# A two-layer graph attention kernel: in layer 1's lightest tiles the norm's mean comes from column sums in the table, the variance from ScalarE, and one row moves from TensorE to VectorE

## The chip, the core and the metric

The program runs on one core of a Trainium2 chip. The metric is the device time of one execution in microseconds (us); lower is better. Several executions are timed and their median is given. The engines are called as the profile calls them: PE (TensorE, matrix products), PEld (its weight loads), DVE (VectorE), ACT (ScalarE), POOL (GpSimd) and SP (SyncE, which only issues DMAs here).

## What is computed

A graph with 10,000 nodes and 170,000 directed edges (80,000 pairs both ways, and one loop per node) goes through two graph attention layers. All numbers are fp32. Layer 1 has four heads of 256 columns, layer 2 one head of 768:

```python
def gat_conv(x, edge_index, W, a_src, a_dst, bias, heads, out_ch, concat):
    xl = (x @ W).reshape(n, heads, out_ch)
    alpha_src = einsum('nhc,hc->nh', xl, a_src)
    alpha_dst = einsum('nhc,hc->nh', xl, a_dst)
    e = leaky_relu(alpha_src[src] + alpha_dst[dst], 0.2)
    e = exp(e - segment_max(e, dst)[dst])
    alpha = e / (segment_sum(e, dst)[dst] + 1e-16)
    return segment_sum(xl[src] * alpha[:, :, None], dst) + bias

h = gat_conv(x, edge_index, W1, a_src1, a_dst1, b1, 4, 256, True)
h = relu(layer_norm(h, g1, be1)) + (x @ Wr1 + br1)
h2 = layer_norm(gat_conv(h, edge_index, W2, a_src2, a_dst2, b2, 1, 768, False), g2, be2)
out = layernorm(x + h2 + (h @ Wr2 + br2))
```

`layer_norm(v, g, b)` is `(v - mean) * rsqrt(var + 1e-5) * g + b` over a node's columns. The change is about the first of the three norms, over 1024 columns.

## The kernel before

**Three stages.** The first stage (lines 590 to 640) makes `table1` in DRAM, one row per node: 1024 columns of `x @ W1` plus `b1`, four destination logits, four source logits, and one number that tells the node's place in the order below. Its loop takes 79 tiles of 128 nodes. For each, PE multiplies (L173), ACT copies the product out of PSUM (L623), DVE multiplies it with the two attention vectors (L626), ACT sums those products by head (L629), POOL adds `b1` (L631) and SP stores the row. A generator, `prepare()`, sorts the nodes by their number of edges in small steps between the tiles. The second stage is layer 1 (`ordered_layer1`), the third layer 2 (`ordered_layer2`).

**Tiles of layer 1.** Nodes are ordered by degree, so each of the 79 tiles of 128 nodes has one number of rows, `SLOTS[t]`: the same number of edges for each of its nodes. Row k of a tile holds, on partition p, the table row of the k-th neighbour of node p. The turns take every second tile from the lightest to the heaviest, then the others back down: 8, 10, 11, 12, 12, 13, 13, 14, 14, 14, 15 (four), 16 (four), 17 (four) and so on up to 26 and 41 rows, then 27 down to 16 (three), 15 (four), 14 (three), 13 (three), 12, 11, 11, 9. In all 1377 rows.

**Gathers.** The rows of a tile are fetched by indirect DMAs that POOL issues (L426), one for each row of 128 nodes, into a ring of 31 rows in SBUF, which is one tile of memory named `ring` in the profile. `ring.fetch` is called as rows are used up, so a row is fetched into the place of the row 31 before it.

**One turn.** The program order is written out by hand (`manual_schedule`), and each engine works through its own part in that order. For tile t:

- Near the end of tile t-1, POOL forms the logits of tile t from the ring (L736) and overwrites the logits in the ring, DVE and ACT turn them into normalised weights `e` (L190, L747, L750, L751, L767, L771 to L773).
- The first `on_pe(t)` rows are PE's: ACT multiplies each by its weights in place (`multiply`, L516, four pieces of 256 columns) and PE adds them up in PSUM with an identity matrix (L728, four records a row). `on_pe` is between 1 and 5: 1 for tiles of up to 13 rows, 2 for 14 and 15, 3 for 16 and 17, 4 for 18 and 19, 5 from 20 on.
- The other rows are DVE's. One in four (the first, the fifth and so on of DVE's rows) DVE weighs itself, with four `scalar_tensor_tensor` of 256 columns (L527). The other three are `shared`: ACT multiplies them (L516, three rows ahead of DVE, `LEAD`), and DVE adds them with one `tensor_tensor` of 1024 columns (L523). Both accumulate in the PSUM tile `acc`; two of these alternate between tiles.
- After the last row comes the norm of tile t, at the head of turn t+1: `deviation` on DVE (two `bn_stats`, L538, one `bn_aggr`, L540) and on ACT (Ln L542, Exp L543, which give 1/sqrt), then on DVE the scaling (L552, L554) and the sum with the residual (L881).
- PE meanwhile transposes x of the tile (L698, copied out by ACT, L699), transposes h of the tile before (L698, L699), multiplies x with `Wr1` (L173) and h with `W2` (L904). ACT copies the last product to `row` (L829) and SP stores it in `table2`.

On PE the order of a turn is therefore L728 (the tile's own rows), L698 (x), L698 (h), L173, L904. On ACT, at the head of a turn, it is Ln, Exp, the two copies L829, the next shared rows, the copies of x, more shared rows, the copies of h.

The function that gives PE its share, and the one that decides which of DVE's rows are shared:

```python
def on_pe(t):
    return min(max(SLOTS[t] // 2 - 5, 1), ON_PE1, SLOTS[t])
...
def shared(t, k):
    return by_vector(t, k) and (k - on_pe(t)) % (SHARE - (len(cuts_of(t)) > 2)) > 0
```

Heavy tiles (22 rows and more) are cut into groups with a running maximum; the change leaves that part as it is.

Of the kernel before, what the change touches and what calls it, by code (L numbers as in the profile page):

```python
# [32 lines left out]
OP = mybir.AluOpType  # L33
# [21 lines left out]
PARTED = 22  # L55

# [25 lines left out]
def gnn_kernel(ctx, tc, x, x_cols, src, dst, src_col, dst_col, W1, a_src1, a_dst1, b1, g1, be1, Wr1, br1,  # L82
# [8 lines left out]
    R1, R2 = C1 + 2 * H1 + 1, C2 + 2 * H2  # L91
# [454 lines left out]
    def scaled(to, parts, mean_and_deviation, g, b):  # L546

        mean, inv = mean_and_deviation
        c = 0
        for a in parts:  # L550
            d = c + a.shape[1]
            nc.vector.scalar_tensor_tensor(to[:, c:d], a, mean, g[:, c:d], op0=OP.subtract, op1=OP.mult)  # L552
            c = d
        nc.vector.scalar_tensor_tensor(to, to, inv, b, op0=OP.mult, op1=OP.add)  # L554
# [13 lines left out]
    with tc.tile_pool(name="w1", bufs=1) as w1p, tc.tile_pool(name="l1", bufs=2) as io, \  # L568
# [22 lines left out]
        nc.scalar.dma_start(b1_b, bass.AP(tensor=b1.tensor, offset=b1.offset, ap=[[0, P], [1, C1]]))  # L591

# [27 lines left out]
        for t in range(NT):  # L620
            p = product(xTs.pop(t), w1, C1)
            row = io.tile([P, R1], F32, name="row")
            nc.scalar.copy(row[:, :C1], p[:, :C1])  # L623
            for i, vec in enumerate((ad_b, as_b)):
                m = io.tile([P, C1], F32, name="scr")
                nc.vector.tensor_mul(m, p[:, :C1], vec)  # L626
                for h in range(H1):
                    s = slice(h * DH1, (h + 1) * DH1)
                    nc.scalar.activation(m[:, s], m[:, s], AF.Copy,  # L629
                                         accum_out=row[:, C1 + i * H1 + h:C1 + i * H1 + h + 1])  # L630
# [45 lines left out]
    def ordered_layer1(mem):  # L676
        nc.scalar.add_instruction(mybir.InstLoadActFuncSet(name=nc.get_next_instruction_name(), act_func_set_id=6, engine=nc.scalar.engine))
        with tc.tile_pool(name="b1", bufs=1) as pool, tc.tile_pool(name="small1", bufs=2) as small, \
# [23 lines left out]
            def from_x(t):  # L702

                xT = pool.tile([P, K0, P], F32, name="xT")
                return xT, halves(xT, xt)

            xt = fetch_x(0)
# [4 lines left out]

            def on_pe(t):


                return min(max(SLOTS[t] // 2 - 5, 1), ON_PE1, SLOTS[t])
# [14 lines left out]
            def summed_logits(lo, hi, ad):  # L731
# [22 lines left out]
            def weights_of(t):  # L754
# [8 lines left out]
                given = summed_logits(at, at + cuts[1], ad)  # L763
# [54 lines left out]

            last = None
# [4 lines left out]
            def store(t):  # L824

                nonlocal full
                row = pool.tile([P, R2], F32, name="row")
# [12 lines left out]
            for t in range(NT + 1):  # L840
# [83 lines left out]
                ahead = iter(())  # L924
                soon = n - LEAD
# [3 lines left out]
                for k in range(n):  # L929
# [20 lines left out]
                    if by_vector(t, k):  # L950
                        weigh(acc, ring.slot(FIRST[t] + k), weights, DH1, shared=shared(t, k))
                    ring.fetch(FIRST[t] + k + 1 + ring.size)
                    due(k)
                due(DEGREES)
                ready += itertools.islice(ahead, max(2 - len(ready), 0))
                last = None
                if live:
                    last = r, acc
# [459 lines left out]
```

## Time and profile before

| | |
|---|---|
| median of three runs | 5525.66 us (5516.87 to 5533.84) |
| the profiled execution | 5484.34 us, span 5482.5 us |
| mean granted TensorE clock in it | 0.944 of full speed |
| instructions | 58273 |
| HBM read, written | 1431.80 MB, 177.29 MB |

The span is the time from the first to the last instruction of the profiled execution. Durations of instructions are read from that execution. The busy digits of the page, in 40 slices of the span (9 is 90% or more), show three stages: the first six slices are the table, the next 18 layer 1, the rest layer 2.

```
DVE  5783343889988888888899995777777777777876
ACT  3434443778889988889888872222222222222322
DMA  4333636899999998999999977988898898888984
```

In a row of the timeline the columns are the start (us), the length, the engine, the line of the kernel, the operation, output and inputs, the shape, and the number of instructions merged; in square brackets stands the time that the engine was idle before, and whom it waited for. A row of groups has the count, then the busy time and the mean length in ns, then the idle time of the engine just before.

### The profile page before, as it was taken

What the parts mean: (1) busy time and instruction counts of PE and PEld (TensorE: products, weight loads), DVE (VectorE), ACT (ScalarE), POOL (GpSimd) and SP (SyncE); (2) the same over time, 40 slices, a digit from 0 to 9 for tenths busy, and PEclk for the clock granted to TensorE, in tenths of its full rate; (3) what the DMA queues carried; (4) which work ended last, traced back from release to release, by engine and by line L of the source; (5) the groups of instructions that cost most, each with busy time, mean ns of one, the idle gap of its engine ahead of it and who ended that gap; (6) DMA issues with size and microseconds to landing.
All of it is one profiled execution on the core that took longest, in us unless ns stands there. A gap on an engine that the chain in (4) does not pass through costs nothing. (4 is left out here: it accounts for less than half of the span.)

```text
span 5482.5 us, 58273 instructions
## 1 busy us (share of the span) xinstructions
PE 4905.3 (89%) x14359; PEld 2707.8 (49%) x14359; DVE 4205.0 (77%) x7341; ACT 2959.9 (54%) x8299; POOL 3341.8 (61%) x3659
## 2 busy tenths in 40 slices
PE   8999995999999987899999997888888888888887
PEld 3444442555544443444445554555555555555554
DVE  5783343889988888888899995777777777777876
ACT  3434443778889988889888872222222222222322
POOL 2446455566667766677676644666666666666663
PEclk9999997999999998999999999989999998988898
DMA  4333636899999998999999977988898898888984
GB/s 156 121 101 90 92 94 216 312 340 363 366 369 377 379 351 291 348 360 384 372 370 363 351 268 261 327 315 309 311 323 313 305 318 304 300 300 301 315 307 168
DMA packets 474303, 1591.30 MB, mean 290 GB/s; under 512 B 118327, under 2 KB 122487, under 8 KB 473958
## 3 DMA queue, kind: packets, MB, share of 16 engines
q0 software_dynamic: 322384, 1286.62, 65.0%
q1 hardware_dynamic: 149520, 297.43, 16.2%
q10 hardware_dynamic: 2054, 3.42, 0.2%
q8 instruction: 122, 2.00, 0.1%
q14 instruction: 223, 1.83, 0.1%
HBM read 1431.80 MB, written 177.29 MB: 293 GB/s over the span
## 5 line engine op out<-in xcount | busy, mean ns | idle before, releaser
L426 POOL DMA_INDIRECT ring<-table,slots x2675 | 2661.1, 995 | 1515.9 <-issue 641.3
L516 ACT ACTIVATE ring<-ring,e 128x256 f32<-128x256 f32 x4232 | 1740.4, 507 | 87.3 <-DVE e L773 49.3
L527 DVE SCALAR_TENSOR_TENSOR acc<-ring,e,acc 128x256 f32<-128x256 f32 (+1 forms) x2574 | 1600.5, 622 | 161.4 <-PE acc L728 72.5
L523 DVE TENSOR_TENSOR acc<-acc,ring 128x1024 f32<-128x1024 f32 x781 | 961.7, 1231 | 66.9 <-ACT ring L516 12.0
L1064 PE MATMUL big<-wr,w 128*128 128x512 f32 (+1 forms) x2464 | 874.6, 499 | 129.8 <-issue 128.0
L1019 PE MATMUL big<-ring,diagonals 128*128 128x256 f32 x2754 | 743.7, 427 | 184.1 <-issue 151.2
L173 PE MATMUL big<-w,xT 128*128 128x512 f32 x1896 | 824.0, 596 | 23.0 <-DMA w<-in_W_dram 10.1
L904 PE MATMUL half<-w,hT 128*128 128x512 f32 (+1 forms) x2528 | 830.4, 486 | 0.0
L173 PE MATMUL big<-wr,xT 128*128 128x512 f32 x1896 | 830.0, 594 | 0.2 <-ACT xT L699 0.2
L1018 ACT ACTIVATE diagonals<-ident,e 128x128 f32<-128x128 f32 x1377 | 422.9, 390 | 641.9 <-PE big L1019 176.2
L1019 PEld LDWEIGHTS big<-ring,diagonals 128*128 128x128 f32 x2754 | 585.6, 216 | 343.2 <-issue 230.4
L1064 PEld LDWEIGHTS big<-wr,w 128*128 128x128 f32 x2464 | 479.9, 196 | 495.6 <-issue 465.8
L904 PEld LDWEIGHTS half<-w,hT 128*128 128x128 f32 x2528 | 477.7, 189 | 372.8 <-issue 331.7
L728 PE MATMUL acc<-ring,ident 128*128 128x512 f32 x1108 | 522.2, 618 | 107.9 <-ACT ring L516 59.8
L173 PEld LDWEIGHTS big<-w,xT 128*128 128x128 f32 x1896 | 361.4, 191 | 481.1 <-issue 463.0
L173 PEld LDWEIGHTS big<-wr,xT 128*128 128x128 f32 x1896 | 355.4, 191 | 418.2 <-issue 417.6
L542 ACT ACTIVATE sd<-mv,eps 128x1 f32<-128x1 f32 x237 | 70.0, 296 | 748.6 <-DVE mv L540 314.6
L728 PEld LDWEIGHTS acc<-ring,ident 128*128 128x128 f32 x1108 | 212.9, 196 | 372.0 <-issue 208.4
L626 DVE TENSOR_TENSOR scr<-big,ad_b 128x1024 f32<-128x1024 f32 x79 | 96.7, 1225 | 374.7 <-ACT row L623 350.9
L631 POOL TENSOR_TENSOR row<-row,none 128x1024 f32<-128x1024 f32 x79 | 187.2, 2370 | 261.4 <-ACT row L623 259.5
L629 ACT ACTIVATE scr<-scr 128x256 f32<-128x256 f32 x632 | 254.5, 404 | 120.3 <-DVE scr L626 120.3
L623 ACT COPY row<-big 128x1024 f32<-128x1024 f32 x79 | 79.7, 1009 | 312.8 <-issue 283.6
(193 smaller groups left out, 3392.8 us busy)
## 6 DMA issues: line engine op xcount, KB each, us to landing
ring<-table,slots POOLq DMA_INDIRECT x2675
table<-row SPq DMA_DIRECT2D x79, 516.0 KB
h_d<-hT SPq DMA_DIRECT2D x79, 512.0 KB
w<-h_d SPq DMA_DIRECT2D x77, 512.0 KB
table<-row SPq DMA_DIRECT2D x79, 385.0 KB
ring<-table SPq DMA_DIRECT2D x79, 385.0 KB
xT<-in_x_cols_dram SPq DMA_DIRECT2D x79, 384.0 KB
x_d<-xt SPq DMA_DIRECT2D x79, 384.0 KB
```

The costliest lines, as they stand in the source:

```text
L173: nc.tensor.matmul(p[:, c:e], aT[:, j, :], w[:, j, c:e], start=(j == 0), stop=(j == k - 1))
L426: nc.gpsimd.indirect_dma_start(out=to, out_offset=None, in_=table, in_offset=bass.IndirectOffsetOnAxis(ap=index, axis=0), **more)
L516: nc.scalar.activation(row[:, s], row[:, s], AF.Copy, scale=e[:, h:h + 1])
L523: nc.vector.tensor_add(acc[:, :c], acc[:, :c], row[:, :c])
L527: nc.vector.scalar_tensor_tensor(acc[:, s], row[:, s], e[:, h:h + 1], (acc if first is None else first)[:, s], op0=OP.mult, op1=OP.add)
L629: nc.scalar.activation(m[:, s], m[:, s], AF.Copy, accum_out=row[:, C1 + i * H1 + h:C1 + i * H1 + h + 1])
L631: nc.gpsimd.tensor_add(row[:, :C1], row[:, :C1], b1_b)
L728: nc.tensor.matmul(acc[:, c:c + BANK], ident, ring.slot(q + k)[:, c:c + BANK], start=(k == 0), stop=(k == m - 1))
L904: nc.tensor.matmul(q, hT[:, j, :], w2[:, j, c:c + q.shape[1]], start=(j == 0), stop=(j == K1 - 1))
L1018: nc.scalar.activation(diagonals[:, (k - lo) % G, :], ident, AF.Copy, scale=e[:, k - lo, :])
L1019: nc.tensor.matmul(to, diagonals[:, (k - lo) % G, :], ring.slot(at + k)[:, ON_PE2:C2], start=False, stop=(k == n - 1), skip_group_check=True)
L1064: nc.tensor.matmul(r[:, c:d], hT[:, j, :], wr2[:, j, c:d], start=False, stop=(j == K1 - 1 and d < C2), skip_group_check=True)
```

## The change

It sets `LIGHTER = 18` and calls a tile *lighter* when it has fewer than 12 rows, or 12, 14 or 16. There are 22 of them: seven of 16 rows, six of 14, three of 12, three of 11, and one each of 10, 9 and 8. Three things change.

1. **The table's rows carry four more columns**, the sums of the row's 256 columns for each head. In the first stage ACT's one copy out of PSUM becomes four, each with an accumulator output, and POOL adds the sums of `b1` to them. A row grows from 1033 to 1037 numbers (4132 to 4148 bytes).
2. **In lighter tiles the norm changes.** POOL copies the sums of a tile's rows out of the ring before they are overwritten, multiplies them by the weights (`mean_begun`), and half way through the tile ACT sums them up to minus the mean (`minus_mean`). After the last row ACT squares `acc` with this mean as bias and sums that up (`deviation_from`), then takes Ln and Exp as before. `bn_stats` and `bn_aggr` fall away. The squares themselves are not needed; they are written over the space of xT and row, which now share one tile of memory, `both`.
3. **In lighter tiles PE gets one row less**, which may leave none. Where none is left, DVE's first row starts the sum with `tensor_scalar` (which does not read `acc`).

```diff
-    R1, R2 = C1 + 2 * H1 + 1, C2 + 2 * H2
+    R1, R2 = C1 + 3 * H1 + 1, C2 + 2 * H2
...
-            nc.scalar.copy(row[:, :C1], p[:, :C1])
+            for h in range(H1):
+                s = slice(h * DH1, (h + 1) * DH1)
+                nc.scalar.activation(row[:, s], p[:, s], AF.Copy,
+                                     accum_out=row[:, C1 + 2 * H1 + h:C1 + 2 * H1 + h + 1])
...
             nc.gpsimd.tensor_add(row[:, :C1], row[:, :C1], b1_b)
+            nc.gpsimd.tensor_add(row[:, C1 + 2 * H1:R1 - 1], row[:, C1 + 2 * H1:R1 - 1], b1_sums)
...
-                xT = pool.tile([P, K0, P], F32, name="xT")
...
+            both = pool.tile([P, D0 + R2], F32, name="both")
+            xT, row, squares = both[:, :D0].rearrange("p (k n) -> p k n", n=P), both[:, D0:], both[:, :C1]
...
+            def lighter(t):
+
+                return SLOTS[t] < LIGHTER and (SLOTS[t] < 12 or SLOTS[t] % 2 == 0)
...
-                return min(max(SLOTS[t] // 2 - 5, 1), ON_PE1, SLOTS[t])
+                return min(max(SLOTS[t] // 2 - 5 - lighter(t), 0), ON_PE1)
...
+                    if sums is not None:
+                        nc.gpsimd.tensor_copy(sums[:, a - lo:b - lo], rows[:, :, C1 + 2 * H1:C1 + 3 * H1])
                     nc.gpsimd.tensor_scalar(slots[:, a:b], rows[:, :, R1 - 1], -1.0, float(NP), op0=OP.mult, op1=OP.min)
                     nc.gpsimd.memset(rows[:, :, C1 + H1:], -BIG)
...
+            def mean_begun(t, e):
+
+                nc.gpsimd.tensor_tensor(sums_of_rows[t], sums_of_rows[t], e, op=OP.mult)
+
+            def minus_mean(t):
+
+                sums = sums_of_rows.pop(t).rearrange("p k h -> p (k h)")
+                mean = small.tile([P, 1], F32, name="mean")
+                nc.scalar.activation(sums, sums, AF.Copy, scale=-1.0 / C1, accum_out=mean)
+                return mean
+
+            def deviation_from(mean, a):
+
+                sd = small.tile([P, 1], F32, name="sd")
+                nc.scalar.activation(squares, a, AF.Square, bias=mean, accum_out=sd)
+                nc.scalar.activation(sd, sd, AF.Ln, scale=1.0 / C1, bias=eps)
+                nc.scalar.activation(sd, sd, AF.Exp, scale=-0.5)
+                return sd
...
-                    r_before, means = last
-                    stats = deviation(small, pieces(means[:, :C1], BANK))
+                    r_before, means, minus = last
+                    if minus is None:
+                        stats = deviation(small, pieces(means[:, :C1], BANK))
+                    else:
+                        stats = minus, deviation_from(minus, means[:, :C1])
...
-                    scaled(h, [means[:, :C1]], stats, g1_b, be1_b)
+                    scaled(h, [means[:, :C1]], stats, g1_b, be1_b, OP.subtract if minus is None else OP.add)
...
+                minus = None
+                if t in sums_of_rows:
+                    mean_begun(t, es[0][0])
...
-                    if by_vector(t, k):
+                    if not k and by_vector(t, k):
+                        for h in range(H1):
+                            s = slice(h * DH1, (h + 1) * DH1)
+                            nc.vector.tensor_scalar(acc[:, s], ring.slot(FIRST[t])[:, s], weights[:, h:h + 1], None,
+                                                    op0=OP.mult)
+                    elif by_vector(t, k):
                         weigh(acc, ring.slot(FIRST[t] + k), weights, DH1, shared=shared(t, k))
                     ring.fetch(FIRST[t] + k + 1 + ring.size)
                     due(k)
+                    if k == n // 2 and t in sums_of_rows:
+                        minus = minus_mean(t)
```

More of the change, by code (lines that the diff above doesn't have):

```diff
@@ L55 @@
 PARTED = 22
+LIGHTER = 18
 def chunk_counts(n_edges):
@@ L551, in scaled @@
             d = c + a.shape[1]
-            nc.vector.scalar_tensor_tensor(to[:, c:d], a, mean, g[:, c:d], op0=OP.subtract, op1=OP.mult)
+            nc.vector.scalar_tensor_tensor(to[:, c:d], a, mean, g[:, c:d], op0=centre, op1=OP.mult)
             c = d
@@ L591, in gnn_kernel @@
         nc.scalar.dma_start(b1_b, bass.AP(tensor=b1.tensor, offset=b1.offset, ap=[[0, P], [1, C1]]))
+        b1_sums = w1p.tile([P, H1], F32, name="b1_sums")
+        nc.vector.reduce_sum(b1_sums, b1_b.rearrange("p (h d) -> p h d", d=DH1), axis=AX.X)
         def weight_steps():
@@ L762, in weights_of @@
                     nc.gpsimd.tensor_copy(ad, own)
-                given = summed_logits(at, at + cuts[1], ad)
+                if lighter(t):
+                    sums_of_rows[t] = small.tile([P, LIGHTER, H1], F32, name="sums", bufs=1)[:, :n]
+                given = summed_logits(at, at + cuts[1], ad, sums_of_rows.get(t))
                 yield
@@ L826, in store @@
                 nonlocal full
-                row = pool.tile([P, R2], F32, name="row")
                 for c, q in full:
@@ L957, in ordered_layer1 @@
                 if live:
-                    last = r, acc
+                    last = r, acc, minus
             store(NT - 1)
```

6 lines of the change are left out of this document (4 added, 2 removed).

## The prediction

> **What bounds the kernel now.** I read the three stages first (the windows view, one row per stage), then single turns of layer 1 in the same view, then the waits, then the timeline of two turns.
>
> ```profile
> PE 4905.3 (89%) x14359; PEld 2707.8 (49%) x14359; DVE 4205.0 (77%) x7341; ACT 2959.9 (54%) x8299; POOL 3341.8 (61%) x3659
> ```
> ```profile
> 0.00:877.00 877.00, 841.59 (x1961) 371.33 (x1961) 482.08 (x979) 355.43 (x1370) 422.00 (x326) 0.99 0.38 107
> 877.00:3320.00 2443.00, 2269.77 (x6582) 1159.29 (x6583) 2126.80 (x3174) 2002.55 (x5064) 1588.32 (x1956) 0.98 0.94 347
> 3320.00:5482.00 2162.00, 1793.93 (x5817) 1177.21 (x5815) 1596.14 (x3188) 601.95 (x1866) 1331.43 (x1377) 0.89 0.86 301
> ```
>
> Columns: stretch, its length, then busy time of PE, PEld, DVE, ACT, POOL, the granted clock, DMA share, GB/s. The first stage (the table) is PE alone: 842 of 877 us. Layer 1, 2443 us, is where the change works; there PE, DVE and the DMA engines are all over 85%, so the averages decide nothing. Layer 2 is untouched. Single turns of layer 1, of 13, 14, 15, 16 and (near the end) 12 rows, cut where L881 ends:
>
> ```profile
> 1074.80:1099.50 24.70, 24.24 (x74) 12.78 (x73) 23.17 (x34) 21.48 (x55) 14.83 (x18) 1.00 0.92 338
> 1099.50:1125.70 26.20, 25.74 (x79) 13.59 (x78) 23.20 (x33) 21.26 (x55) 15.86 (x19) 1.00 0.93 344
> 1206.80:1233.60 26.80, 25.83 (x78) 13.59 (x78) 25.11 (x38) 21.86 (x56) 17.64 (x24) 1.00 0.94 347
> 1314.40:1342.50 28.10, 27.64 (x84) 14.39 (x83) 25.32 (x38) 22.99 (x60) 19.04 (x25) 1.00 0.97 364
> 3227.90:3251.20 23.30, 22.84 (x68) 12.11 (x68) 21.83 (x33) 17.03 (x44) 13.80 (x17) 1.00 0.87 307
> ```
>
> From 13 to 14 rows the turn grows by 1.5 us while DVE's work does not grow (23.17, 23.20); from 14 to 15 DVE grows by 1.9 and the turn by 0.6. So two clocks run side by side and the later one sets each turn. The waits of DVE in two 14-row turns, then in three 16-row turns (total, times, longest):
>
> ```profile
> DVE acc L527 <- PE acc L728: 3.1, 2, 1.6
> ```
> ```profile
> DVE acc L527 <- PE acc L728: 3.2, 3, 1.1
> ```
>
> Even sizes wait for TensorE's sum of its own rows (L728): 1.57 us a turn at 14 rows, 1.07 at 16. The 15-row turns have no such wait. Without the wait DVE alone would need 26.3 - 1.57 = 24.75 us (14 rows), 28.0 - 1.07 = 26.93 (16), 24.65 (13), 26.8 (15), 23.3 (12): I call this DVE's clock. PE's clock follows from its timeline in a 14-row turn:
>
> ```profile
> 1123.66 3.60 PE L728 MATMUL acc<-ring,ident 128*128 128x512 f32 x8
> 1127.10 0.82 PE L698 MATMUL half<-ident,xt 128*128 128x128 f32 x6
> 1128.37 1.09 PE L698 MATMUL half<-ident,h 128*128 128x128 f32 x8 [0.46 <-ACT xT L699]
> ```
>
> Two rows take 1127.10 - 1123.66 = 3.44 us, so one row 1.72. PE's clock is 26.3 us with two rows; hence 24.6 with one, 28.0 with three, and 22.9 with none if only PE's own work counted.
>
> **The change part by part.** 22 turns are "lighter": 7 of 16 rows, 6 of 14, 3 of 12, 3 of 11, one each of 10, 9 and 8. Each loses one PE row: -1.72 us of PE.
>
> *The row goes to DVE.* By the sharing rule (every fourth DVE row is weighed by DVE itself, the others are weighed by ScalarE and only added), the extra row is an added one for 16, 12, 11, 10 and 8 rows, and a weighed one for 14 and 9. Their prices stand in the 13-row turn:
>
> ```profile
> 1074.75 2.06 DVE L527 SCALAR_TENSOR_TENSOR acc<-ring,e,acc 128x256 f32<-128x256 f32 x4
> 1076.90 3.88 DVE L523 TENSOR_TENSOR acc<-acc,ring 128x1024 f32<-128x1024 f32 x3
> ```
>
> Weighed: 2.06 us. Added: 3.88 / 3 = 1.29.
>
> *The norm leaves DVE, partly.* The end of a 14-row turn on DVE, and ACT beside it:
>
> ```profile
> 1117.55 2.49 DVE L523 TENSOR_TENSOR acc<-acc,ring 128x1024 f32<-128x1024 f32 x2
> 1120.07 1.30 DVE L538 BATCH_NORM_STATS2 st<-acc 128x6 f32<-128x512 f32 x2
> 1121.72 1.28 DVE L552 SCALAR_TENSOR_TENSOR h<-acc,mv,g 128x1024 f32<-128x1024 f32 x1
> 1123.11 1.28 DVE L554 SCALAR_TENSOR_TENSOR h<-h,sd,be 128x1024 f32<-128x1024 f32 x1
> 1124.50 1.22 DVE L881 SCALAR_TENSOR_TENSOR h<-h,big 128x1024 f32<-128x1024 f32 x1
> 1127.30 1.01 DVE L527 SCALAR_TENSOR_TENSOR acc<-ring,e,acc 128x256 f32<-128x256 f32 x2 [1.57 <-PE acc L728]
> ```
> ```profile
> 1117.71 3.31 ACT L516 ACTIVATE ring<-ring,e 128x256 f32<-128x256 f32 x8 [1.16 <-DVE total L772]
> 1121.65 0.30 ACT L542 ACTIVATE sd<-mv,eps 128x1 f32<-128x1 f32 x1 [0.62 <-DVE mv L540]
> 1121.98 0.20 ACT L543 ACTIVATE sd<-sd 128x1 f32<-128x1 f32 x1
> ```
>
> From the last add (1120.04) to L552 are 1.68 us of statistics. They go. In their place ScalarE squares acc, and the question is whether L552, which reads the same acc, may run beside it. The first stage answers by analogy: DVE's L626 and ACT's L623 both only read the product, and L626 needs nothing that L623 writes.
>
> ```profile
> 604.74 0.40 ACT L629 ACTIVATE scr<-scr 128x256 f32<-128x256 f32 x1
> 605.05 0.19 ACT L629 ACTIVATION_READ_ACCUMULATOR scr<-scr 128x1 f32 x1
> 609.92 1.01 ACT L623 COPY row<-big 128x1024 f32<-128x1024 f32 x1 [4.68 <-issue]
> ```
> ```profile
> 610.97 1.22 DVE L626 TENSOR_TENSOR scr<-big,ad_b 128x1024 f32<-128x1024 f32 x1 [7.94 <-ACT row L623]
> ```
> ```profile
> L802 ACT COPY ring<-acc 128x1024 f32<-128x1024 f32 x13 | 13.1, 1006 | 14.5 <-remote 8.4 <-PE half L904 4.3 <-PE acc L728 1.2
> ```
>
> L626 starts 0.04 after L623 ends: two engines' reads of one PSUM tile are put one after the other. So L552 will wait for the square. Its length is not in the trace; bounds are 1.01 (the copy of acc, L802) and 1.3 (that plus a separate accumulator read of 0.19 and 0.1 more for a bias held per partition, the difference of L542 and L543). I take 1.11 + 0.09 for the end of the read + 0.07 for two handovers: L552 starts 1.27 after the last add instead of 1.68. **DVE gains 0.41 us, not 1.68.** The deviation (0.30 + 0.20) is ready before L552 ends. If L552 need not wait, L554 would wait for it instead, at about 1.85 + 0.1: a gain of 1.1. The other end, a square that starts late because ACT is still weighing rows, is a rival below.
>
> The Trainium skill, "PSUM — Partial Sum Buffer", section "PSUM bank collisions raise a hardware error", says that accesses by two engines to one bank collide, reads against reads included, so software has to keep them apart. By it L552 waits, as in the L626 row; it speaks against the reading that the whole of the statistics comes off DVE. By it layer 1 comes out at +1.6 (below), without it at -8.0.
>
> *Tiles of 12 rows and under: no PE row is left.* What then follows the big product L904 on PE is the transposition of x, whose copies ACT makes. From the 13-row turn, where one row is left (L904 ends as L728 starts):
>
> ```profile
> 1072.79 1.88 PE L728 MATMUL acc<-ring,ident 128*128 128x512 f32 x4
> 1075.79 1.09 PE L698 MATMUL half<-ident,h 128*128 128x128 f32 x8 [0.46 <-ACT xT L699]
> ```
> ```profile
> 1072.99 0.38 ACT L829 COPY row<-half 128x258 f32<-128x258 f32 x1 [1.23 <-PE half L904]
> 1073.26 1.71 ACT L516 ACTIVATE ring<-ring,e 128x256 f32<-128x256 f32 x4
> 1075.15 0.86 ACT L699 COPY xT<-half 128x512 f32<-128x512 f32 x2 [0.17 <-PE half L698]
> ```
>
> ACT stands idle only 0.17 us before the xT copies: copy, four multiplications (row 1 now, row 2 before) and xT copies stay in this order. So without L728 the copies come only 0.17 earlier, and PE's clock goes from 24.6 to 24.4, not to 22.9.
>
> *The sum for layer 1*, later clock of the two, in us:
> 16 rows: PE 28.0 to 26.3, DVE 26.93 + 1.29 - 0.41 = 27.81; 28.02 to 27.81 = -0.2, x7 = -1.5.
> 14 rows: PE 26.3 to 24.6, DVE 24.75 + 2.06 - 0.41 = 26.4; +0.1, x6 = +0.6.
> 12 and under: DVE at most 23.5 + 0.9 = 24.4, PE 24.6 to 24.4; -0.17, x9 = -1.5.
> That is -2.4. But several light turns run on DVE's clock already, because PE had a lead when they came (the 12-row turn of 23.30 above); there the dearer DVE turn counts in full. Carrying both clocks through the 78 turns in order (rows start when L881 and L728 are done; the transposition of h starts when L881 and PE's own work are done) gives **+1.6**; with no gain on DVE at all it gives +7.9, with 1.1 of gain -8.0, and without the ACT chain at 1.1 -16.6.
>
> *The table.* Four pieces with accumulator (4 x 0.40 + 0.09) replace one copy of 1.01: 0.7 us later for L626, hidden behind DVE's 7.94 us of idle time, except for the last tile, whose row layer 1 awaits: **+0.7**. The sum of b1 lies in DVE's idle time before its first product. *Rows of 4148 bytes instead of 4132*, 0.39%, count where the DMA engines are full, in the two stretches of 17 to 21 rows:
>
> ```profile
> 1399.00:1891.60 492.60, 475.38 (x1389) 242.56 (x1388) 438.82 (x617) 437.08 (x1107) 346.01 (x410) 1.00 0.99 374
> 2401.20:2887.30 486.10, 470.59 (x1381) 240.65 (x1379) 437.81 (x619) 432.16 (x1098) 343.94 (x406) 1.00 1.00 377
> ```
>
> PE is 97% busy in both, so 0 if PE sets them and 0.39% of 979 = 3.8 if the DMA engines do; I take **+1**. The outer bound is 0.39% of 2443 = 9.5. *POOL*: a copy and a product a light turn, some 0.3 us each, inside this gap at the turn's head or beside the gathers:
>
> ```profile
> 1126.29 1.00 POOL L426 DMA_INDIRECT ring<-table,slots  x1 [4.46 <-issue]
> ```
>
> Nothing; without that cover 22 x 0.6 = 13. The mean on ACT (some 0.4 us) lies in its idle time. **Sum: +1.6 + 0.7 + 1 = +3 us** on the profiled 5484.3, 5488. That execution is 41 us under the median of the runs, 5525.7; for the median I forecast 5529.
>
> **The rivals.**
> *DVE has room and the whole PE row comes off.* 22 turns at up to 1.72, carried through: -35 us, 5491. For it: PE is the later clock in the even sizes. Against it: 15-row turns, with two PE rows and 25.11 us of DVE, take 26.8, so the 16-row turn with two PE rows cannot take 26.3. Chance 0.14.
> *The square comes late (slower).* ACT is in order, and at the end of a turn it weighs the next turn's PE rows: in the 14-row turn those eight end at 1121.02, 0.98 after the last add. Beyond 1.68 - 1.27 = 0.41 of lateness the new norm costs DVE more than the old. At 1.4 of lateness each light turn loses 1.0 against before plus its row: carried through, +26, with the rest 5554. Against it: one PE row less is four weighings (1.65 us) less in just that place. Chance 0.13.
> *xT, row and squares share one tile.* If the xT copies had to wait for the store of row that was issued just before them, every turn of the 78 would be late by at least that store:
>
> ```profile
> table<-row SPq DMA_DIRECT2D x79, 385.0 KB
> ```
>
> At 344 GB/s 1.1 us, so +87 or more, 5613. Against it: the gathers wait for single slots of the ring, which is one tile too. Chance 0.03.
>
> **How the numbers follow.** Forecast 5529, chance 0.70; its own range, from the bounds of -8 and +8 and 9 us of scatter between runs, is 5515 to 5545. The range that should hold 8 in 10 also takes in half of each near rival: 5508 to 5552. Less than 0.3% (16.6 us) is about what a measurement of this kernel can tell from no change; so faster 0.14, same 0.70, slower 0.16.
>
> **What would show it.** In the profile after: L527's wait for L728 gone or under 0.4 us in 14- and 16-row turns; 14-row turns still near 26.3, 16-row turns near 27.8; L552 preceded by a wait for the square of about 1.2 us; in turns of 11 and 12 rows ACT without a gap before the xT copies; layer 2 unchanged. I am wrong if L552 starts right behind the last add, if a light turn falls below 25.5 (14) or 27 (16), or if heavy turns, which the change does not touch, get longer by more than 0.1 us.

## The result and the profile after

| | before | after |
|---|---|---|
| median of 22 runs each | 5525.74 us | 5535.95 us |
| lowest and highest | 5512.24, 5540.83 | 5528.04, 5550.54 |
| the profiled execution | 5484.34 us | 5532.32 us |

The ratio is 1.0020, 95% interval 1.0013 to 1.0027: the change costs about 10 us (7 to 15). The two profiled executions lie 48 us apart, but that is no measure of the change: that of before lies 41 us under its median, that of after 4 us. Layer 2, whose code is unchanged, is some 20 us longer in the second (2163.7 us before, 2183.7 after, from the last L881 or L920 on; the profiles of the eight runs on one chip below lie between 2157.7 and 2175.5). So sizes of whole stages are taken from medians, and the traces are used for what is the same in every turn.

The windows view of the three stages after (stretch, length, busy time of PE, PEld, DVE, ACT, POOL, granted clock, DMA share, GB/s):

```profile
0.00:890.00 890.00, 843.35 (x1958) 371.68 (x1961) 482.86 (x977) 396.73 (x1914) 436.21 (x403) 0.99 0.38 105
890.00:3345.50 2455.50, 2237.80 (x6492) 1144.73 (x6493) 2125.70 (x3153) 2016.24 (x5132) 1608.69 (x2009) 0.97 0.94 346
3345.50:5530.40 2184.90, 1818.08 (x5819) 1192.24 (x5817) 1598.08 (x3190) 597.88 (x1866) 1332.67 (x1377) 0.88 0.85 298
```

In layer 1 PE has lost 32 us of work (2269.77 to 2237.80: 22 rows of 1.72 would be 38) and DVE has gained none on balance (2126.80 to 2125.70), yet the stage is not shorter: in this profile it is 12 us longer, chiefly in turns that the change does not touch (see the bytes and POOL, below). In the first stage ACT has grown by 41 us (355.43 to 396.73), and the first turn of layer 1 ends 13 us later (L920 at 964.4; L881 at 951.1 before). That end alone is no measure: among the runs below it comes between 955.7 and 961.2 in the five whose first stage has the tile period of before, and at 973.3 in the run of the table alone. PE's waits in the middle of that stage (40 to 270 us; waiting line, what it waited for, total, times, longest), before and then after:

```profile
PE big L173 <- PE big L173: 6.6, 8, 0.9
...
PE big L173 <- DVE scr L626: 1.0, 1, 1.0
```
```profile
PE big L174 <- DVE scr L632: 16.1, 11, 1.5
```

After, PE waits there for DVE to finish with a product (L632), 1.5 us a tile. Before it waited 0.9 a tile; the profile puts one of those nine waits down to DVE (L626) and eight to PE's own product before. The prediction put no cost on that stage but the last tile.

Single turns of layer 1 after: 13, 14, 15 and 16 rows.

```profile
1088.40:1113.00 24.60, 24.14 (x77) 12.85 (x76) 23.11 (x35) 19.72 (x51) 15.36 (x20) 1.00 0.92 339
1139.80:1166.20 26.40, 24.21 (x74) 12.75 (x74) 23.56 (x35) 21.00 (x56) 17.02 (x21) 1.00 0.93 325
1219.90:1246.70 26.80, 25.81 (x78) 13.59 (x78) 25.11 (x38) 21.02 (x54) 16.98 (x23) 1.00 0.95 337
1328.20:1356.00 27.80, 27.49 (x78) 14.43 (x78) 24.87 (x36) 23.38 (x60) 19.15 (x27) 0.94 0.98 360
```

The 14-row turn takes 26.4 and the 16-row turn 27.8. The turns of 13 and 15 rows, which the change leaves alone, stand where they were (24.6, 26.8). The end of a 14-row turn on DVE, and ACT beside it:

```profile
1132.39 2.06 DVE L528 SCALAR_TENSOR_TENSOR acc<-ring,e,acc 128x256 f32<-128x256 f32 x4
1135.77 1.28 DVE L553 SCALAR_TENSOR_TENSOR h<-acc,mean,g 128x1024 f32<-128x1024 f32 x1 [1.32 <-ACT both L851]
...
1138.56 1.22 DVE L920 SCALAR_TENSOR_TENSOR h<-h,big 128x1024 f32<-128x1024 f32 x1
1139.70 0.48 DVE L528 SCALAR_TENSOR_TENSOR acc<-ring,e,acc 128x256 f32<-128x256 f32 x1
```
```profile
1134.54 1.11 ACT L851 ACTIVATE both<-acc,mean 128x1024 f32<-128x1024 f32 x1 [1.53 <-PE half L943]
1135.55 0.19 ACT L851 ACTIVATION_READ_ACCUMULATOR both<-acc,mean 128x1 f32 x1
```

The square (L851) takes 1.11 us and starts 0.09 after DVE's last row (1134.45); ACT had been idle for 1.53, so it is not late (the bracket names PE's L943, but the start fits the end of DVE's row). L553 (L552 before) waits for it: 1.32 us instead of 1.68 of statistics. Right behind L920 the next tile's rows start without a gap: the wait for PE's sum is gone.

### The profile page after: what moved, and what is told of

The parts are those of the page before. It is cut to its first block, busy times and chain, and to the rows that moved or that the text cites. A ratio compares the mean times of both kernels' runs of the same rounds, so it can differ in the third digit from the quotient of the medians.

```text
span 5530.4 us, 58913 instructions
## 1 busy us (share of the span) xinstructions
PE 4899.2 (89%) x14268; PEld 2708.6 (49%) x14271; DVE 4206.6 (76%) x7319; ACT 3010.9 (54%) x8912; POOL 3377.6 (61%) x3789
## 5 line engine op out<-in xcount | busy, mean ns | idle before, releaser
L528 DVE SCALAR_TENSOR_TENSOR acc<-ring,e,acc 128x512 f32<-128x512 f32 (+1 forms) x2566 | 1596.4, 622 | 124.7 <-PE acc L740 31.5
L524 DVE TENSOR_TENSOR acc<-acc,ring 128x1024 f32<-128x1024 f32 x796 | 980.2, 1231 | 89.9 <-ACT ring L517 27.3
L1068 PE MATMUL big<-ring,diagonals 128*128 128x256 f32 x2754 | 759.6, 433 | 198.3 <-issue 173.6
L174 PE MATMUL big<-wr,both 128*128 128x512 f32 x1896 | 838.6, 599 | 0.2 <-ACT both L706 0.2
L943 PE MATMUL half<-w,hT 128*128 128x512 f32 (+1 forms) x2528 | 830.5, 486 | 0.0
L943 PEld LDWEIGHTS half<-w,hT 128*128 128x128 f32 x2528 | 477.5, 189 | 373.1 <-issue 334.8
L174 PEld LDWEIGHTS big<-wr,both 128*128 128x128 f32 x1896 | 359.0, 193 | 423.8 <-issue 423.1
L740 PE MATMUL acc<-ring,ident 128*128 128x512 f32 x1020 | 474.9, 612 | 69.0 <-ACT ring L517 48.6
L632 DVE TENSOR_TENSOR scr<-big,ad_b 128x1024 f32<-128x1024 f32 x79 | 96.7, 1224 | 371.6 <-ACT row L628 264.3
L740 PEld LDWEIGHTS acc<-ring,ident 128*128 128x128 f32 x1020 | 193.2, 194 | 310.6 <-issue 171.3
L628 ACT ACTIVATE row<-big 128x256 f32<-128x256 f32 x316 | 116.5, 382 | 286.6 <-issue 245.8
```

Source lines behind the costliest of these rows:

```text
L174: nc.tensor.matmul(p[:, c:e], aT[:, j, :], w[:, j, c:e], start=(j == 0), stop=(j == k - 1))
L524: nc.vector.tensor_add(acc[:, :c], acc[:, :c], row[:, :c])
L528: nc.vector.scalar_tensor_tensor(acc[:, s], row[:, s], e[:, h:h + 1], (acc if first is None else first)[:, s], op0=OP.mult, op1=OP.add)
L740: nc.tensor.matmul(acc[:, c:c + BANK], ident, ring.slot(q + k)[:, c:c + BANK], start=(k == 0), stop=(k == m - 1))
L943: nc.tensor.matmul(q, hT[:, j, :], w2[:, j, c:c + q.shape[1]], start=(j == 0), stop=(j == K1 - 1))
L1068: nc.tensor.matmul(to, diagonals[:, (k - lo) % G, :], ring.slot(at + k)[:, ON_PE2:C2], start=False, stop=(k == n - 1), skip_group_check=True)
```

## The experiments

Two theories stood against each other. **First stage:** the cost comes from the four copies with accumulator, which stand in a ring of waits between DVE and ACT. **Light turns:** it comes from the turns of layer 1, where the row costs DVE more than the norm gives back. A third one, the longer rows of the table, was tried by itself. Ratios are to the kernel before on the same chip; 0.0010 is 5.5 us.

**The table alone: no tile is lighter.** The sums are made and stored, and nobody uses them; the shared tile `both` stays.

```diff
-LIGHTER = 18
+LIGHTER = 0
...
-                return min(max(SLOTS[t] // 2 - 5 - lighter(t), 0), ON_PE1)
+                return min(max(SLOTS[t] // 2 - 5, 1), ON_PE1, SLOTS[t])
```

> The changed kernel with no lighter tile: the table keeps its four sum columns, ACT keeps the four pieces with accumulator, xT and row keep their shared tile, and layer 1's turns are those of before. Theory (the first stage pays): in the profile of the changed kernel the end of the first L881 (there L920) came 13 us later than before, because in the stretch where DVE also searches the sorted list, the tile's period grew from 11.45 to 12.01 us: ACT's copy out of PSUM lies on the chain there. Then this run should be 8 to 13 us over before, with the first turn's end at 964, and light turns as before (14 rows at 26.3, 16 at 28.0). Rival (the lighter turns pay, the first stage is scatter): within 3 us of before, and the period in that stretch back at 11.45.

Measured: 5507.94 against 5490.89, 1.0026 (1.0014 to 1.0039): +14 us (8 to 21). PE's waits in its first stage are those of after:

```profile
PE big L174 <- DVE scr L632: 16.1, 11, 1.5
```

That is about the whole of the change's cost, and a little over the range expected. The first turn ends at 973.3, later than the 964 expected.

**The longer rows alone.** The kernel before with rows of 4148 bytes, the four new columns filled with zeros by POOL.

```diff
-    R1, R2 = C1 + 2 * H1 + 1, C2 + 2 * H2
+    R1, R2 = C1 + 3 * H1 + 1, C2 + 2 * H2
...
+            nc.gpsimd.memset(row[:, C1 + 2 * H1:R1 - 1], 0.0)
```

> Before with rows of 4148 bytes, the four new columns set to zero and not used. Theory (the gathers' bytes cost next to nothing): first stage as before, layer 1 longer by 0 to 4 us, in all 0 to +4. Rival (the longer rows are what made turns 38 to 50 some 10 us longer in the changed kernel's profile): +8 to +12, in the turns of 20 rows and more.

Measured: 5494.74 against 5490.89, 1.0009 (0.9998 to 1.0020). The bytes cannot be told from nothing; up to 11 us are not excluded by this ratio alone. But the two stretches of 17 to 21 rows, where the DMA engines are full and longer rows would show first, hold still:

```profile
1407.30:1899.50 492.20, 475.87 (x1390) 242.76 (x1389) 438.69 (x617) 435.81 (x1109) 347.76 (x410) 1.00 0.99 376
2409.80:2897.10 487.30, 470.72 (x1381) 240.52 (x1379) 437.83 (x619) 430.97 (x1098) 345.25 (x407) 1.00 0.99 377
```

492.2 and 487.3 us, against 492.6 and 486.1 before.

**The sums off the chain.** After, but the copy is one again, and ACT forms the sums from the finished row, behind POOL's addition of `b1`; so POOL's addition of the sums of `b1` falls away.

```diff
-            for h in range(H1):
-                s = slice(h * DH1, (h + 1) * DH1)
-                nc.scalar.activation(row[:, s], p[:, s], AF.Copy,
-                                     accum_out=row[:, C1 + 2 * H1 + h:C1 + 2 * H1 + h + 1])
+            nc.scalar.copy(row[:, :C1], p[:, :C1])
...
+            for h in range(H1):
+                s = slice(h * DH1, (h + 1) * DH1)
+                nc.scalar.activation(m[:, s], row[:, s], AF.Copy,
+                                     accum_out=row[:, C1 + 2 * H1 + h:C1 + 2 * H1 + h + 1])
```

> The changed kernel, but the first stage has its one copy out of PSUM back; the sums are formed by ACT afterwards, from the row with b1 already added, in four passes with accumulator behind the sums of the logits. ACT has 0.65 us more to do in each of the 79 tiles than in the changed kernel. Theory (only the place on the chain mattered): the period in the search stretch is 11.45 again, the first turn ends at 951 to 953, and the time is 8 to 12 us under the changed kernel: -2 to +4 against before. Rival (ACT's load or POOL's extra work mattered, not the chain): no better than the changed kernel, +10.

Measured: 5496.08 against 5490.89, 1.0016 (1.0002 to 1.0029). PE's waits are back to the pattern of before, although ACT does more work here than in after:

```profile
PE big L174 <- PE big L174: 6.5, 8, 0.9
...
PE big L174 <- DVE scr L627: 1.0, 1, 1.0
```

So it was the place of the pieces that cost, not their amount. What is left, 9 us by the ratio (1 to 16) and 5 by the medians, is the light turns' share and the bytes. Both lie over the -2 to +4 expected, which the interval does not rule out.

**The row alone.** The kernel before with `lighter` and the row moved, and the norm as before.

```diff
-                return min(max(SLOTS[t] // 2 - 5, 1), ON_PE1, SLOTS[t])
+                return min(max(SLOTS[t] // 2 - 5 - lighter(t), 0), ON_PE1)
...
-                    if by_vector(t, k):
+                    if not k and by_vector(t, k):
+                        for h in range(H1):
+                            s = slice(h * DH1, (h + 1) * DH1)
+                            nc.vector.tensor_scalar(acc[:, s], ring.slot(FIRST[t])[:, s], weights[:, h:h + 1], None,
+                                                    op0=OP.mult)
+                    elif by_vector(t, k):
```

> Before with one row moved from PE to DVE in the 22 lighter tiles, and the norm and table as before. Theory (two clocks, DVE's is the later once the row is moved): 16-row turns at 26.93 + 1.29 = 28.2 us, 14-row turns at 24.75 + 2.06 = 26.8, 12-row turns at 24.6; carried through all turns +8 us. Rival (PE is the bound and DVE has room): 16 rows at 26.8, 14 rows at 25, in all -15 to -35.

Measured: 5495.70 against 5490.89, 1.0011 (0.9999 to 1.0022), +6 us (-1 to 12). The turns are the better witness, a 14-row and a 16-row one:

```profile
1130.00:1156.80 26.80, 24.30 (x74) 12.75 (x74) 25.11 (x39) 19.56 (x51) 16.84 (x19) 1.00 0.93 324
1319.40:1347.60 28.20, 25.89 (x78) 13.50 (x78) 26.42 (x40) 22.78 (x60) 19.14 (x24) 1.00 0.99 359
```

DVE is 1.6 us busier in the first than in after (25.11 against 23.56), and the turn is 0.4 longer: that is what the new norm is worth, because 1.32 of the 1.68 us remain as a wait.

**The norm alone**, on the kernel with the sums off the chain: `on_pe` as before, the norm as after.

```diff
-                return min(max(SLOTS[t] // 2 - 5 - lighter(t), 0), ON_PE1)
+                return min(max(SLOTS[t] // 2 - 5, 1), ON_PE1, SLOTS[t])
```

> As e3 (sums off the chain), but with PE's rows as before: only the norm of the lighter tiles is changed. Theory (two clocks; in even sizes PE is the later one): 14-row turns stay at 26.3 and 16-row turns at 28.0, because the 0.4 us off DVE is spent waiting for L728; carried through all turns -1 us in layer 1, so 0 to +4 against before with the first stage of e3. Rival (the statistics are worth their 1.5 us wherever they go): 22 x 1.5 = -33.

Measured: 5496.52 against 5490.93, 1.0006 (0.9995 to 1.0018). DVE's waits in turns 1 to 17, before and then here:

```profile
DVE acc L527 <- PE acc L728: 18.3, 11, 4.7
```
```profile
DVE acc L528 <- PE acc L738: 18.2, 12, 4.8
DVE h L553 <- issue: 8.9, 5, 2.1
```

With PE's row in its place PE still sets these turns, so nothing that the norm does on DVE can count. And L553 waits 2.1 us in a 14-row turn. The profile names no releaser for that wait ("issue"), but L553 starts at 1132.08, 0.03 after the end of the accumulator read behind the square. The square is late there, on ACT:

```profile
1127.65 3.31 ACT L517 ACTIVATE ring<-ring,e 128x256 f32<-128x256 f32 x8 [0.99 <-DVE e L787]
1130.86 1.10 ACT L849 ACTIVATE both<-acc,mean 128x1024 f32<-128x1024 f32 x1
```

Eight weighings for PE's two rows hold it up by 0.8 us. This is the second rival's late square, hidden here behind PE; in after the row's move takes four of the eight away.

**Two halves, swapped between the engines.** On the kernel with the sums off the chain: ACT squares the first 512 columns while DVE scales the last 512, then they change places.

```diff
-                nc.scalar.activation(squares, a, AF.Square, bias=mean, accum_out=sd)
...
+                nc.scalar.activation(squares[:, lo], a[:, lo], AF.Square, bias=mean, accum_out=first)
+                nc.vector.scalar_tensor_tensor(to[:, hi], a[:, hi], mean, g1_b[:, hi], op0=OP.add, op1=OP.mult)
+                nc.scalar.activation(first, first, AF.Identity, scale=1.0 / C1, bias=eps)
+                nc.scalar.activation(squares[:, hi], a[:, hi], AF.Square, bias=mean, accum_out=sd)
+                nc.vector.scalar_tensor_tensor(to[:, lo], a[:, lo], mean, g1_b[:, lo], op0=OP.add, op1=OP.mult)
+                nc.scalar.activation(sd, sd, AF.Ln, scale=1.0 / C1, bias=first)
...
-                    scaled(h, [means[:, :C1]], stats, g1_b, be1_b, OP.subtract if minus is None else OP.add)
...
+                        nc.vector.scalar_tensor_tensor(h, h, inv, be1_b, op0=OP.mult, op1=OP.add)
```

> As e3, but ACT squares the first half of acc (one PSUM bank) while DVE scales the second half, and then the other way round; the two sums are put together with one more ACT instruction of one column. Theory (L552 waits because both engines would read one bank): DVE's wait of 1.32 us before L552 falls under 0.2, a shorter wait of about 0.7 appears before L554, a 14-row turn falls from 26.43 to 26.1 and a 16-row turn from 27.80 to 27.5; 6 us under e3. Rival (the tile as a whole is what is guarded, or the wait is for the deviation): the wait stays at 1.3 or moves to L554 in full, time as e3.

Measured: 5505.39 against 5490.93, 1.0032 (1.0022 to 1.0043), and a miss: slower than with whole squares, by 9 us. DVE and ACT at the end of a 16-row turn:

```profile
1317.17 0.75 DVE L852 SCALAR_TENSOR_TENSOR h<-acc,mean,g 128x512 f32<-128x512 f32 x1 [0.91 <-ACT both L851]
```
```profile
1316.36 0.69 ACT L851 ACTIVATE both<-acc,mean 128x512 f32<-128x512 f32 x1
1316.95 0.19 ACT L851 ACTIVATION_READ_ACCUMULATOR both<-acc,mean 128x1 f32 x1
...
1318.01 0.69 ACT L854 ACTIVATE both<-acc,mean 128x512 f32<-128x512 f32 x1 [0.54 <-DVE h L852]
```

DVE's L852 reads columns 512 to 1023, ACT's L851 the others, and L852 still starts 0.02 us after the accumulator read behind L851 (1316.95 + 0.19 = 1317.14, and 1317.17). The two reads of one tile are put one after the other whether they touch the same columns or not, and now there are two such handovers a turn. The 14-row turn goes from 26.4 to 27.1, the 16-row turn from 27.8 to 28.5. The Trainium skill, "PSUM — Partial Sum Buffer", section "PSUM bank collisions raise a hardware error", says that engines on different banks do not collide; the halves of `acc` are 2048 bytes each, one bank by that page. By it the halves could run side by side; here the program waited for the tile as a whole, 0.91 us, and no run shows whether the chip needed it.

**The step moved.** The kernel before, with the generator's step of a tile put behind the copy instead of at the end of the tile. So ACT's sum of a weight product (L609) comes behind the copy (L623) in ACT's order.

```diff
             nc.scalar.copy(row[:, :C1], p[:, :C1])
+            if t:
+                next(steps, None)
...
-            next(steps, None)
```

> Before, with one change of order in the first stage: the sorting and weight steps are issued after the next tile's copy out of PSUM instead of ahead of it. ACT's copy then no longer queues behind the weight step's sum (0.86 us), which waits for DVE. Theory (DVE's step, ACT's sum, ACT's copy and DVE's product are one ring, and its length sets the stretch): the period of 14 tiles falls from 11.45 to 10.3 to 10.6, 12 to 16 us under before. Rival (DVE's own work sets the stretch, 11.45 is its busy time): no change, within 3 us of before.

Measured: 5470.63 against 5490.93, 0.9957 (0.9941 to 0.9973): 20 us faster than before (15 to 32), by the line order alone, and more than the 12 to 16 expected. ACT and PE in that stretch:

```profile
160.71 1.01 ACT L623 COPY row<-big 128x1024 f32<-128x1024 f32 x1 [4.69 <-issue]
161.62 0.85 ACT L609 ACTIVATE scr<-scr 128x768 f32<-128x768 f32 x1
```
```profile
149.74 24.62 PE L173 MATMUL big<-w,xT 128*128 128x512 f32 x57
```

57 matrix products without a gap, 24 a tile: 10.3 us a tile instead of 11.45.

**Everything together:** sums off the chain, the step moved, the halves, and in tiles without a PE row ACT's shared rows behind the copies of x.

```diff
-                multiplied(first + 2)
+                if not live or first:
+                    multiplied(first + 2)
```

> The changed kernel with the sums off the chain (e3), the halves swapped (e6), the steps moved (e7), and in tiles without a PE row the copies of x ahead of the weighing of row 1 on ACT. Expected by the chain theory: e3's first stage less 12 to 16, layer 1 less 6 for the halves and less 3 for the order (PE's wait of 1.6 us for the copies of x gone in the tiles of 12 rows and under, whose turns come to 23 to 24): 12 to 20 us under before. By the rivals above: as e3.

Measured: 5490.35 against 5490.93, 0.9998 (0.9986 to 1.0010). A miss (12 to 20 us under before were expected), and most of it follows from the two runs before it: the kernel with the halves lay 14 us over before, and the step gains 20. The new order on ACT did little: PE's wait for the copies of x in the last turns falls from 7.4 us to 0.5, but turns 62 to 78 take 442.0 us against 443.2 with the halves alone.

**The norm on the odd sizes.** The norm alone and the step moved, with the tiles of 13, 15 and 17 rows as the lighter ones; PE keeps its rows.

```diff
-                return SLOTS[t] < LIGHTER and (SLOTS[t] < 12 or SLOTS[t] % 2 == 0)
+                return SLOTS[t] in (13, 15, 17)
```

> The norm change where DVE's clock is the later one: tiles of 13, 15 and 17 rows get the mean from the sums and the squares on ACT, all tiles keep PE's rows of before; sums off the chain and steps moved as in e3 and e7. Theory (each DVE-bound turn gets the 0.36 us that the norm really saves, until PE's clock holds it): 15-row turns from 26.81 to 26.45, 17-row turns from 28.19 to about 28.0, 13-row turns stay at 24.6; layer 1 -4 us, with e7's first stage 20 to 26 us under before. Rival (the norm is worth the whole of its statistics): 15-row turns at 26.3 and 17-row turns at 28.0 as well, since PE holds both, so the two differ only in the 15-row turn by 0.15 us.

Measured, on another chip, where before takes 5162.02: 5142.58, 0.9963 (0.9949 to 0.9976). A turn of 15 rows, which runs on DVE's clock:

```profile
2938.50:2964.90 26.40, 25.84 (x78) 13.59 (x78) 23.56 (x35) 22.77 (x59) 18.73 (x27) 1.00 0.98 358
```

26.4 where the run below, on the same chip with these turns unchanged, takes 26.8: DVE has 1.6 us less work (25.11 there) and the turn gets 0.4 of it. The 17-row turns come to 27.95, about the 28.0 expected. The time is 19 us under before where 20 to 26 were expected. The step alone gave the same ratio within its interval, so nothing is measurable beyond that.

**After with the step moved**, behind its four pieces.

```diff
                                      accum_out=row[:, C1 + 2 * H1 + h:C1 + 2 * H1 + h + 1])
+            if t:
+                next(steps, None)
...
-            next(steps, None)
```

> The changed kernel with one change of order in the first stage, the steps issued after the next tile's pieces (as e7). The four pieces with accumulator stay. Theory (the pieces cost only because they stand in the ring of step, sum, copy and product): the stretch runs at 10.3 us a tile, the first turn ends at 938 to 942 instead of 964, and what is left against before is e7's gain plus the lighter turns' +6: 8 to 16 us under before. Rival (four pieces and POOL's additions load the stage in any order): a period over 10.6 and a time at or over before.

Measured, on the same chip as the run before: 5142.03 against 5162.02, 0.9962 (0.9949 to 0.9976). That is 20 us under before (12 to 26), more than the 8 to 16 expected. The change itself, with one call moved, beats the kernel before by as much as that call alone does without the change. Its 15-row turn, and PE's waits between 40 and 270 us, which have no line of DVE's products left; the line shown is the only wait of a table product:

```profile
2941.30:2968.10 26.80, 25.80 (x78) 13.59 (x78) 25.11 (x39) 21.08 (x55) 17.22 (x23) 1.00 0.99 370
```
```profile
PE big L174 <- ACT row L617: 1.0, 1, 1.0
```

So the four pieces are free once nothing waits behind them in a ring, as the first theory says. What the light turns cost (below) is smaller than the width of the two intervals and cannot be read from these two ratios.

## Why the prediction was right in its range and wrong in its reason

The time forecast, 5529, lies 7 us under the 5536 measured; the change costs 10 us where +3 was said. The turns of 14 and 16 rows came out as worked out; the larger part of the cost came from a place that the prediction called hidden. So the time fell into the range of 5515 to 5545 partly by luck: that range was made for doubts about layer 1 and for scatter between runs, and had nothing in it for this place.

**The two clocks: right.** Forecast 26.4 us for 14 rows and 27.81 for 16; measured 26.4 and 27.8 in the rows above. The row's prices on DVE (2.06 weighed, 1.29 added) hold: with the row alone the turns are 26.8 and 28.2, and 24.75 + 2.06 = 26.81, 26.93 + 1.29 = 28.22. The rival in which the whole PE row comes off is dead.

**L552 waits for the square: right.** 1.27 was said, 1.32 measured. So DVE gains 0.36 us, not 0.41, and the 15-row turn of the odd-size run shows just that. The late square did not come: ACT was idle before it in the 14-row turn above, since the row's move had taken its four weighings away from there, as the prediction argued; without the move it was late. The shared tile held nothing up either: the 13- and 15-row turns are unchanged.

**Twelve rows and under: the mechanism right, the sum too small.** ACT goes through copy, shared rows and copies of x without a gap, and PE waits for it, as said. In a turn of 11 rows on ACT, then PE:

```profile
1013.44 0.38 ACT L865 COPY both<-half 128x258 f32<-128x258 f32 x1 [2.89 <-PE half L943]
1013.71 1.71 ACT L517 ACTIVATE ring<-ring,e 128x256 f32<-128x256 f32 x4
1015.32 0.84 ACT L706 COPY both<-half 128x512 f32<-128x512 f32 x2
```
```profile
1015.94 1.09 PE L705 MATMUL half<-ident,h 128*128 128x128 f32 x8 [1.63 <-ACT both L706]
```

What was missed is that DVE, now with more rows, waits for the same queue: its next shared rows stand behind the copies of x. DVE's waits in the last stretch of layer 1 (2900 to 3345 us):

```profile
DVE h L553 <- ACT both L851: 10.7, 8, 1.4
DVE acc L524 <- ACT ring L517: 3.9, 7, 1.1
```

Before, the second kind came to 0.4 us there, once.

**The light turns: +1.6 said, more measured.** From the end of one turn's last DVE step (L881, L920) to another's, turns 1 to 17 take 447.2 us after and 447.4 before; turns 62 to 78 take 437.4 and 431.5. That is +5.7. In the second stretch PE had a lead before, and its three 14-row turns show the loss; the second of them and the sum of the three, before, then after:

```profile
3103.30:3127.90 24.60, 24.14 (x71) 12.68 (x71) 23.11 (x33) 21.30 (x54) 14.66 (x18) 1.00 1.01 389
...
sum 76.60, PE 75.56 PEld 40.00 DVE 69.50 ACT 61.62 POOL 48.15; mean PE 25.19 PEld 13.33 DVE 23.17 ACT 20.54 POOL 16.05
```
```profile
3127.30:3153.70 26.40, 24.21 (x74) 12.75 (x74) 23.56 (x35) 20.99 (x55) 17.04 (x21) 1.00 0.98 364
...
sum 80.00, PE 75.75 PEld 40.12 DVE 70.90 ACT 62.68 POOL 50.49; mean PE 25.25 PEld 13.37 DVE 23.63 ACT 20.89 POOL 16.83
```

The second goes from 24.6, which is PE's work and no wait, to 26.4, DVE's clock. 76.6 become 80.0, so 3.4 of the 5.7 us are here: DVE's dearer turn counts in full where the PE row cost nothing. The prediction named this, and sized it too small. The kernels with the row moved that were profiled (the sums off the chain, the row alone, after with the step moved) take 436 to 439 us for turns 62 to 78; those with PE's rows in place 430 to 432.

With PE's row gone PE now stands idle for about 2 us in many light turns, mostly waiting for L920. Right after four of these waits the profile after shows the granted clock at half for 3.4 us (before, turns 62 to 78 have no such stretch and a clock of 1.00). It costs nothing that shows: the 16-row turn above at a clock of 0.94 takes 27.8 us like its neighbours at 1.00, and in the three 14-row turns just shown DVE never waits for PE.

**The table: this step failed.** The prediction held the four pieces to be "hidden behind DVE's 7.94 us of idle time, except for the last tile", +0.7. That idle time is that of a tile at 605 us, where `prepare()` gives DVE little. And it read the stage as PE alone, from 842 busy us of 877; in part of the tiles that does not hold. Between about 50 and 265 us DVE works on the search for the order and on the weight products, and stands in a ring with ACT. Before, on DVE and ACT, one tile:

```profile
161.89 0.95 DVE L608 TENSOR_TENSOR scr<-w,a 128x768 f32<-128x768 f32 x1
164.74 1.23 DVE L626 TENSOR_TENSOR scr<-big,ad_b 128x1024 f32<-128x1024 f32 x1 [1.90 <-ACT row L623]
```
```profile
162.87 0.84 ACT L609 ACTIVATE scr<-scr 128x768 f32<-128x768 f32 x1 [5.01 <-DVE scr L608]
...
163.71 0.99 ACT L623 COPY row<-big 128x1024 f32<-128x1024 f32 x1
```

ACT must sum DVE's weight product (L609) before it may copy the next table product, and DVE's next step waits for that copy. The product has long been there; the ring is DVE's step, 0.84 + 0.99 of ACT, and round again, 11.45 us a tile where PE needs 10.3. After, the same place, DVE, ACT and PE:

```profile
155.63 0.95 DVE L611 TENSOR_TENSOR scr<-w,a 128x768 f32<-128x768 f32 x1
159.04 1.23 DVE L632 TENSOR_TENSOR scr<-big,ad_b 128x1024 f32<-128x1024 f32 x1 [2.46 <-ACT row L628]
```
```profile
156.61 0.84 ACT L612 ACTIVATE scr<-scr 128x768 f32<-128x768 f32 x1 [5.02 <-DVE scr L611]
...
157.45 0.36 ACT L628 ACTIVATE row<-big 128x256 f32<-128x256 f32 x1
...
158.79 0.22 ACT L628 ACTIVATION_READ_ACCUMULATOR row<-big 128x1 f32 x1
```
```profile
149.64 10.54 PE L174 MATMUL big<-w,xT 128*128 128x512 f32 x24 [1.47 <-DVE scr L632]
161.65 10.54 PE L174 MATMUL big<-w,xT 128*128 128x512 f32 x24 [1.47 <-DVE scr L632]
```

From the first piece to the end of the last accumulator read are 1.56 us instead of 0.99, and all of it lands in the period: 161.65 - 149.64 = 12.01, so 0.56 a tile more than 11.45. By PE's waits shown under the result that is 16.1 - 6.6 - 1.0 = 8.5 us for the stretch; 14 tiles of it by 0.56 are 7.8. The term was 0.7 and measured about 8. The period repeats from profile to profile: 11.45 us before and in the five runs that leave the copy whole and the step in its place, 12.01 after and in the table alone, 10.3 in the four runs with the step moved.

**The bytes and POOL: not contradicted.** The longer rows show nothing that a run here can tell from nothing, and turns of 17 rows take 28.2 us before and after. But one sign of being wrong that the prediction named did show in this one profile: heavy turns, which the change does not touch, got longer. Turns 18 to 61 (17 rows and more) take 1497.8 us after and 1488.8 before, and the 9 us are all in turns 38 to 49. The other profiles do not bear it out: turns 18 to 61 take 1486.3 us with the sums off the chain, whose layer 1 is the same as in after, and 1489.8 with the longer rows alone. So they are counted here as scatter of one execution; what made it is not known.

**What stays open.** First stage (about 8) and light turns (about 6) make 14 by the traces; the medians give 10 (7 to 15). The runs of the parts, +14 (8 to 21) for the table and +9 (1 to 16) for the rest, agree with that only at their lower ends. How the 10 us split is therefore known to some 4 us, not better. That the first stage has the larger part rests on the run of the table alone and on the one with the step moved.

## What to carry to other kernels

Slack is that of a place, not of an engine: before a step is called hidden, look at the idle time in every stretch of the loop in which the step runs, above all where another generator's work is woven in. In an in-order queue, what was issued before a copy is part of the copy's latency; moving one call behind it was worth twice what the whole change cost. And where two engines read one PSUM tile in turn, moving statistics from one to the other only gains the difference of their lengths.

## What the runs showed of the hardware

Reads of one PSUM tile by DVE and ACT were put one after the other here even where they touch different halves of it (the wait of 0.91 us above). Cutting an ACT copy of 1024 columns (0.99 us) into four of 256 with accumulator made it 1.56: each piece takes 0.36 to 0.39, and its accumulator read 0.19 to 0.22, of which about half runs beside the piece.
